# Moving the untaken branch for extra expert blocks one step ahead in a latent-attention and mixture-of-experts kernel

## The chip, the cores and the metric

The kernel runs on one core of a Trainium2 chip. The metric is the device time of one execution in microseconds (us); a value is the median of several runs. PE is TensorE, DVE is VectorE, ACT is ScalarE, POOL is GpSimd, and SP is the queue that mostly issues transfers.

## The reference

The input x has 2 x 4096 tokens of 512 channels in float32. It is normalized without gain, xn = layernorm(x). Two branches read xn, and both are added to x:

```python
x = x + attn(xn) + ffn(xn)

# attn: 64-channel latent attention, causal, one head
c  = (xn @ W_to_kv.T) @ W_compress.T
ch = layernorm(c) * ln_gamma + ln_beta
q, k, v = ch @ W_q_comp.T, *split(ch @ W_kv_comp.T)      # rotary on q and k
o  = softmax(causal(q @ k.T / 8)) @ v
z  = o @ W_comp2lat.T
attn = z @ W_to_kv + z @ W_out_res.T + b_out_res

# ffn: 16 experts, the best 2 for each token, and one shared expert
p   = softmax(xn @ router_w.T); w, e = top_k(p, 2); w = w / sum(w)
ffn = silu(xn @ shared_gate) * (xn @ shared_up) @ shared_down
ffn[token] += w * ((silu(xn @ gate[e]) * (xn @ up[e])) @ down[e])
```

## The kernel before, in words

The kernel has five stages. (1) In 16 groups of 512 tokens it normalizes, routes, computes the shared expert, and projects q, k and v; the rows of xn go to the DRAM buffer xn_d, the shared part to acc_d. (2) It sorts the tokens by expert through DRAM. (3) Attention for six pairs of query blocks (FIRST) runs. (4) The expert stage runs, and within it some scores for a further pair. (5) Attention for the other pairs (REST) runs, together with the summing of all parts into the output.

*The expert stage.* Each token stands twice in the sorted order, which is cut into blocks of 128 rows. There are at most 143 blocks (NBLK): 98 lie in 49 pairs of one expert, the other 45 are single. The last six single blocks (NTAIL) are needed only when the routing is unusually uneven, so they stand inside a branch on a count, `used`. The 137 usual blocks are done in 69 steps (`n_usual`, steps 0 to 68) of two blocks each; as 39 usual singles is an odd number, the last step, 68, has only one block. For step t these helpers are traced:

- `fetch` (three weight transfers of 512 KB each, issued by SP) and `gather_for` (POOL gathers 128 rows of xn_d for each block);
- `x_T`: PE transposes the rows into the PSUM tiles pxt (L1026), DVE copies them to xt and computes the row weight sw (L1029 to L1034);
- `gate_up`: PE multiplies into the PSUM pair pg (L1052), ACT takes silu (esg, L1057), DVE the product (eh, L1058);
- `down`: PE multiplies into the PSUM pair py (L1066), ACT scales the rows by sw into y (L1070) and issues the store to y_d (L1071).

The order on PE, DVE and ACT is the order in which the source traces the work; a scheduler only adds the waits. The loop body is, shortened:

```python
fetch_for(t + 2); gather_for(...); gate_up(t)
...
down(t - 1)
exps(1)                 # a waiting exponential of attention, on ACT
x_T(t + 2)
```

so that `gate_up` of a step always stands ahead of `down` of the step before. After the last `down` every engine loads `used` (L1099) and jumps over the branch (L1101). An untaken branch still ends on each engine with an event by which the others know that it has passed; those that come to a buffer that was used inside the branch wait for it. On SP and POOL that end also waits for earlier transfers.

*Buffers.* PSUM pairs (`psA`) rotate between two buffers and serve pg, py, the scores s and the sums po. In SBUF the pools wx (weights, gathered rows) and ex (a fourth weight buffer, xt, esg, eh, y) are released after the expert stage. In their place come the pool rb for tiles E, which hold rows of scores, and the pool fin for the summing.

*Attention (REST).* For each turn PE transposes pieces of E into the PSUM tiles et (L857), ACT or DVE copies them to eT (L863 to L866), PE multiplies with v into oT (L877); meanwhile PE computes scores s for the next pair (L804), DVE scales them into E and takes the maximum (L812, L809), and ACT takes exponentials in place (L820). Tiles E come from rb, 8 buffers, and when 8 are live from ring_k, 4 buffers. For summing, SP loads acc_d rows into fac (L1141), POOL gathers rows of y_d by position onto fac or into fyy (L1146), and DVE adds (L1167, L1176). These loads and gathers need all stores to y_d.

## Time and profile before

| | |
|---|---|
| runs | 2016.24, 2014.66, 2008.76 us |
| median | 2014.66 us |
| profiled execution | 2016.73 us, its span 2014.9 us |
| mean granted TensorE clock | 0.971 |
| PE busy | 1907.1 us (95%) |
| DVE, ACT, POOL busy | 1057.6, 650.0, 572.9 us |

The profile is of one execution. Its span runs from the first to the last instruction; the time of the run has 1.8 us more. Times in rows count from the span's start. A q behind an engine's name is its sequencer, which waits, branches and issues; "idle before" is the time in which the engine did nothing before the row, with the one that ended it. In these times the expert stage runs up to about 1676, and attention for the other pairs from there to the end.

### The profile page before, as it was taken

How to read it: one execution, taken by the hardware profiler on the slowest of the kernel's cores; microseconds unless marked ns; L12 is line 12 of the kernel's file. 1: busy time of each engine (PE TensorE's matmuls, PEld its weight loads, DVE VectorE, ACT ScalarE, POOL GpSimd, SP SyncE). 2: the span in 40 equal slices, each digit the busy share in tenths (PEclk: the TensorE clock that was granted, in tenths of full speed). 3: DMA queues.
4: the chain of work that ended last, by engine and by line, in shares of the span. 5: the costliest groups of instructions: out<-in, count | busy, mean ns of one | idle time of the engine just before them, and what ended most of it. 6: DMA issues, size and time to landing. Idle time of an engine off the chain costs nothing. (4 is left out here: it accounts for less than half of the span.)

```text
span 2014.9 us, 33391 instructions
## 1 busy us (share of the span) xinstructions
PE 1907.1 (95%) x13010; PEld 1402.0 (70%) x13010; DVE 1057.6 (52%) x2882; ACT 650.0 (32%) x1097; POOL 572.9 (28%) x499
## 2 busy tenths in 40 slices
PE   7999999999999898889999999999999998999997
PEld 6877777777777777467777777777777674444544
DVE  8777777776767677642222322222223315677775
ACT  2222222222222222551111111111111354666665
POOL 2333333333333234101111111111111105555552
PEclk9999999999999998999999999999999999999999
DMA  6221212121212121427887878887877767889885
GB/s 229 63 74 63 74 63 74 64 74 64 74 63 74 64 74 48 147 72 238 271 277 264 300 247 282 281 279 264 276 275 242 243 231 179 216 206 218 201 209 141
DMA packets 219440, 342.50 MB, mean 170 GB/s; under 512 B 19204, under 2 KB 109952, under 8 KB 219280
## 3 DMA queue, kind: packets, MB, share of 16 engines
q1 hardware_dynamic: 167600, 234.09, 35.5%
q0 software_dynamic: 31696, 69.99, 13.8%
q10 hardware_dynamic: 19984, 36.25, 4.7%
q8 instruction: 104, 1.70, 0.4%
q14 instruction: 56, 0.46, 0.1%
HBM read 250.22 MB, written 90.05 MB: 169 GB/s over the span
## 5 line engine op out<-in xcount | busy, mean ns | idle before, releaser
L1052 PE MATMUL pg<-xt,wgu 128*128 128x256 f32 (+1 forms) x2816 | 497.1, 336 | 0.0
L1052 PEld LDWEIGHTS pg<-xt,wgu 128*128 128x128 f32 x2816 | 435.5, 191 | 43.3 <-issue 0.5
L995 POOL DMA_INDIRECT xg<-xn_d,table x137 | 131.4, 959 | 692.7 <-DVE sw L1034 545.5
L1058 DVE TENSOR_TENSOR eh<-esg,pg 128x512 f32<-128x512 f32 (+1 forms) x69 | 47.2, 684 | 399.4 <-ACT esg L1057 393.6
L1066 PE MATMUL py<-wdn,eh 128*128 128x512 f32 x548 | 247.1, 594 | 0.0
L1029 DVE COPY xt<-pxt 128x512 f32<-128x512 f32 x138 | 88.4, 682 | 182.3 <-PE pxt L1026 182.3
L1066 PEld LDWEIGHTS py<-wdn,eh 128*128 128x128 f32 x548 | 102.2, 190 | 106.6 <-issue 98.5
L812 DVE TENSOR_SCALAR_CACHE_REDUCE E<-s 128x512 f32<-128x512 f32 x224 | 144.6, 687 | 58.5 <-PE s L804 39.5
L1070 ACT ACTIVATE y<-py,sw 128x512 f32<-128x512 f32 x137 | 94.2, 688 | 231.4 <-PE py L1066 203.0
L820 ACT ACTIVATE E<-E,nb 128x1024 f32<-128x1024 f32 (+7 forms) x160 | 160.7, 1007 | 20.9 <-DVE nb L815 20.7
L1057 ACT ACTIVATE esg<-pg 128x512 f32<-128x512 f32 (+1 forms) x69 | 41.0, 594 | 370.9 <-PE pg L1052 304.6
L804 PE MATMUL s<-kT,qT 64*128 64x512 f32 (+2 forms) x576 | 144.2, 590 | 16.4 <-DVE E L812 12.6
L877 PE MATMUL oT<-eT,vv 128*64 128x256 f32 (+1 forms) x1088 | 146.7, 392 | 1.4 <-DVE qT L879 0.6
L423 POOL DMA_INDIRECT order_d<-tok,at_u x128 | 126.3, 987 | 64.5 <-issue 36.4
L863 ACT COPY eT<-et 128x512 f32<-128x512 f32 x190 | 104.2, 587 | 110.3 <-PE et L857 63.4
L877 PEld LDWEIGHTS oT<-eT,vv 128*64 128x64 f32 x1088 | 67.3, 138 | 91.5 <-issue 35.0
L857 PEld LDWEIGHTS et<-ident,E 64*128 64x128 f32 x2112 | 81.8, 140 | 70.1 <-issue 49.2
L384 POOL TENSOR_TENSOR x<-x,b_bc 128x2048 f32<-128x2048 f32 x16 | 76.0, 4751 | 186.2 <-DVE xn L381 173.4
L458 PE MATMUL plc<-RC,xnT 128*64 128x80 f32 x1024 | 72.3, 288 | 48.1 <-ACT xnT L447 36.6
L1146 POOL DMA_INDIRECT fyy<-y_d,pos_all x64 | 82.4, 1288 | 121.2 <-PE s L804 54.2
L857 PE MATMUL et<-ident,E 64*128 64x64 f32 x2112 | 101.9, 231 | 15.4 <-ACT E L820 8.4
L1146 POOL DMA_INDIRECT fac<-y_d,pos_all x64 | 98.7, 1541 | 62.2 <-DMA fac<-y_d,pos_all 51.5
(246 smaller groups left out, 2830.2 us busy)
## 6 DMA issues: line engine op xcount, KB each, us to landing
wgu<-in_L_ffn_gate_w_dram SPq DMA_DIRECT2D x88, 512.0 KB
wgu<-in_L_ffn_up_w_dram SPq DMA_DIRECT2D x88, 512.0 KB
wdn<-in_L_ffn_down_w_dram SPq DMA_DIRECT2D x88, 512.0 KB
y_d<-y ACTq DMA_DIRECT2D x137, 256.0 KB
xn_d<-xn SPq DMA_DIRECT2D x16, 1028.0 KB
x<-in_L_attn_x_dram SPq DMA_DIRECT2D x16, 1024.0 KB
acc_d<-x SPq DMA_DIRECT2D x16, 1024.0 KB
fac<-acc_d SPq DMA_DIRECT2D x64, 256.0 KB
```

Source lines behind the costliest of these rows:

```text
L423: G.indirect_dma_start(out=order_d[n % 4], out_offset=bass.IndirectOffsetOnAxis(ap=at_u[:, i, k:k + 1], axis=0), in_=tok[:, g * 4 + i, k:k ...
L804: mm(out=sc[b][:, 0:w], lhsT=q[e, :], rhs=kT[c][e, 0:w], start=True, stop=True)
L812: V.tensor_scalar(dst, sc[b][:, 0:w], SCALE, None, ALU.mult, ALU.max, accum_out=m)
L820: S.activation(E, E, AF.Exp, bias=nb[:, b:b + 1], accum_out=sm[:, b, c:c + 1])
L857: tr(pt[h][:, o:o + H], rows[i][j // 8][e, b, (j % 8) * P:(j % 8 + 1) * P], ident[e, e])
L863: copy(dst[:, h:h + 3:2, :], pt[h].rearrange("p (u c) -> p u c", u=2))
L877: mm(out=o, lhsT=vv[j // 4][:, b, j % 4, :], rhs=e, start=(j == 0), stop=(j == n - 1))
L995: G.indirect_dma_start(out=x_n, out_offset=None, in_=xn_d, in_offset=bass.IndirectOffsetOnAxis(ap=table[:, n:n + 1], axis=0))
L1052: mm(out=pg[:, g, f, at_s], lhsT=weights[u][0][:, c, g * FE + f * P:g * FE + (f + 1) * P], rhs=x_u[:, c, :], start=(c == 0), stop=(c == 3))
L1066: mm(out=py[:, v, :], lhsT=hT[:, c, v * P:(v + 1) * P], rhs=weights[u][1][:, c, :], start=(c == 0), stop=(c == 1))
L1070: S.activation(y, py[:, v, :], AF.Copy, scale=slot_w.pop(n))
L1146: G.indirect_dma_start(out=y, out_offset=None, in_=y_d, in_offset=bass.IndirectOffsetOnAxis(ap=pos[k][:, j:j + 1], axis=0), compute_op=ALU ...
```

## The change

The branch moves into step 68. There, `down(67)` is traced first, then the branch, then `gate_up(68)` and `down(68)`. The branch's six blocks are now six steps of one block instead of three of two. Inside it the weights have a tile tag of their own (wgu_l), and the down weights and transposed rows take tiles of the gathered rows' tag. In step 68 a second block's rows are scaled on DVE and stored by SP. The pool rb of 8 buffers becomes rb of 5 and rc of 3.

```diff
-    tail = [flow[n:n + 2] for n in range(0, len(flow), 2)]
+    tail = [[f] for f in flow]
...
+    def row_tile(name):
+        return wx.tile([P, D + TOPK], F32, tag="xg", name=name, bufs=GBUFS)[:, 0:D]
...
-    def fetch(u):
+    def fetch(u, late=False):
...
-        pool, bufs = (wx, WBUFS) if k < WBUFS else (ex, 1)
-        wgu = pool.tile([P, 4, 2 * FE], F32, tag="wgu", name=f"wgu{u}", bufs=bufs)
-        wdn = pool.tile([P, 2, D], F32, tag="wdn", name=f"wdn{u}", bufs=bufs)
+        pool, bufs = (wx, WBUFS) if k < WBUFS and not late else (ex, 1)
+        wgu = pool.tile([P, 4, 2 * FE], F32, tag="wgu_l" if late else "wgu", name=f"wgu{u}", bufs=bufs)
+        if late:
+            wdn = [row_tile(f"wdn{u}_{c}") for c in range(2)]
+        else:
+            wdn_all = pool.tile([P, 2, D], F32, tag="wdn", name=f"wdn{u}", bufs=bufs)
+            wdn = [wdn_all[:, c, :] for c in range(2)]
...
         def x_T(t):
-            xt = ex.tile([P, 4, 2, P], F32, tag="xt", name=f"xt{t}")
+            xt = (ex.tile([P, 4, 2, P], F32, tag="xt", name=f"xt{t}") if t < n_usual
+                  else row_tile(f"xt{t}").rearrange("p (c v t) -> p c v t", c=4, v=1))
...
                 y = ex.tile([P, D], F32, tag="y", name=f"y{n}", bufs=4)
+                if t == n_usual - 1 and v:
+                    V.tensor_scalar(y, py[:, v, :], slot_w.pop(n), None, ALU.mult)
+                    nc.sync.dma_start(out=y_d[n * P:(n + 1) * P, :], in_=y)
+                    continue
                 S.activation(y, py[:, v, :], AF.Copy, scale=slot_w.pop(n))
                 S.dma_start(out=y_d[n * P:(n + 1) * P, :], in_=y)
+
+        def last_blocks():
+            more_than_usual = nc.values_load(used[0:1, 0:1], min_val=0, max_val=NBLK, ...)
+            with tc.If(more_than_usual > NBLK - NTAIL):
+                for t in range(n_usual, len(steps2)):
+                    for u, _ in steps2[t]:
+                        fetch(u, True)
+                    gather_for(t, True)
+                    x_T(t)
+                    gate_up(t)
+                    down(t)
...
+                if t == n_usual - 1:
+                    down(t - 1)
+                    last_blocks()
                 gate_up(t)
...
-            if t:
+            if t and t != n_usual - 1:
                 down(t - 1)
...
-        more_than_usual = nc.values_load(used[0:1, 0:1], ...)
-        with tc.If(more_than_usual > NBLK - NTAIL):
-            for t in range(n_usual, len(steps2)):
...
-    rb_ = ctx.enter_context(tc.tile_pool(name="rb", bufs=8))
+    rb_ = ctx.enter_context(tc.tile_pool(name="rb", bufs=5))
+    rc_ = ctx.enter_context(tc.tile_pool(name="rc", bufs=3))
...
-        pool = rb_ if sum(t[0] is rb_ for t in live) < 8 else ring_k
+        pool = next(q for q, k in ((rb_, 5), (rc_, 3), (ring_k, 4)) if sum(t[0] is q for t in live) < k)
```

More of the change, by code (lines that the diff above doesn't have):

```diff
@@ L979, in fetch @@
             in_=up_w[bass.ds(e, 1), :, :].rearrange("e (c p) f -> p (e c) f", p=P))
-        nc.sync.dma_start(
-            out=wdn,
-            in_=down_w[bass.ds(e, 1), :, :].rearrange("e (c p) f -> p (e c) f", p=P))
+        if late:
+            for c in range(2):
+                nc.sync.dma_start(
+                    out=wdn[c], in_=down_w[bass.ds(e, 1), c * P:(c + 1) * P, :].rearrange("e p f -> p (e f)"))
+        else:
+            nc.sync.dma_start(
+                out=wdn_all,
+                in_=down_w[bass.ds(e, 1), :, :].rearrange("e (c p) f -> p (e c) f", p=P))
         weights[u] = wgu, wdn
@@ L1065, in down @@
                 for c in range(2):
-                    mm(out=py[:, v, :], lhsT=hT[:, c, v * P:(v + 1) * P], rhs=weights[u][1][:, c, :],
+                    mm(out=py[:, v, :], lhsT=hT[:, c, v * P:(v + 1) * P], rhs=weights[u][1][c],
                        start=(c == 0), stop=(c == 1))
@@ L1069, in down @@
                 y = ex.tile([P, D], F32, tag="y", name=f"y{n}", bufs=4)
+                if t == n_usual - 1 and v:
+                    V.tensor_scalar(y, py[:, v, :], slot_w.pop(n), None, ALU.mult)
+                    nc.sync.dma_start(out=y_d[n * P:(n + 1) * P, :], in_=y)
+                    continue
                 S.activation(y, py[:, v, :], AF.Copy, scale=slot_w.pop(n))
                 S.dma_start(out=y_d[n * P:(n + 1) * P, :], in_=y)
+        def last_blocks():
+            more_than_usual = nc.values_load(used[0:1, 0:1], min_val=0, max_val=NBLK,
+                                             skip_runtime_bounds_check_because="a sum of block counts that cannot exceed NBLK")
+            with tc.If(more_than_usual > NBLK - NTAIL):
[6 more added lines that the diff above has]
+                    down(t)
         rows, todo = score_steps(E_first, NPA, two_banks)
@@ L1096, in tile_mla_then_moe @@
                 (offsets_of_tokens if t == 20 else slots)()
-        more_than_usual = nc.values_load(used[0:1, 0:1], min_val=0, max_val=NBLK,
-                                         skip_runtime_bounds_check_because="a sum of block counts that cannot exceed NBLK")
-        with tc.If(more_than_usual > NBLK - NTAIL):
-            for t in range(n_usual, len(steps2)):
-                for u, _ in steps2[t]:
-                    fetch(u)
-                gather_for(t, True)
-                x_T(t)
-                gate_up(t)
-                down(t)
     on_way.__exit__(None, None, None)
-    rb_ = ctx.enter_context(tc.tile_pool(name="rb", bufs=8))
+    rb_ = ctx.enter_context(tc.tile_pool(name="rb", bufs=5))
+    rc_ = ctx.enter_context(tc.tile_pool(name="rc", bufs=3))
     fin = ctx.enter_context(tc.tile_pool(name="fin", bufs=2))
```

## The prediction

> **What bounds the kernel now.** I read the page's busy row first, then everything that names the branch's line, then PE, ACT and DVE in order of time around it. Columns of a timeline row: start, length, engine, line, operation, count, and in brackets the idle time before it and what ended it.

> ```profile
> PE 1907.1 (95%) x13010; PEld 1402.0 (70%) x13010; DVE 1057.6 (52%) x2882; ACT 650.0 (32%) x1097; POOL 572.9 (28%) x499
> L1070 ACT ACTIVATE y<-py,sw 128x512 f32<-128x512 f32 x137 | 94.2, 688 | 231.4 <-PE py L1066 203.0
> ```

> TensorE is the bound: time is won or lost only where PE stands. The second row counts 137 scaled row blocks, all 143 but the last six, so the branch is not taken in this run: only its test and its joining are paid.

> ```profile
> L1101 SPq EVENT_SEMAPHORE  x9: 17/17/17, 1653.8 to 1678.1; - x9
> ...
> L1101 DVEq COMPARE_BRANCH  x1: 72/72/72, 1670.1 to 1670.1; - x1
> ...
> L1101 PEldq COMPARE_BRANCH  x1: 3346/3346/3346, 1670.6 to 1670.6; - x1
> ...
> L1101 ACTq EVENT_SEMAPHORE  x1: 17/17/17, 1676.6 to 1676.6; - x1
> ...
>   DVE E L812: 8.4, 1
> ```

> PE's jump took 3346 ns, DVE's 72. SP comes out of the branch only at 1678.1, ACT at 1676.6, and DVE had to wait for SP.

> ```profile
> 1661.89 3.60 PE L1066 MATMUL py<-wdn,eh 128*128 128x512 f32 x8
> 1665.33 3.73 PE L1052 MATMUL pg<-xt,wgu 128*128 128x128 f32 x32
> 1668.90 5.32 PE L1066 MATMUL py<-wdn,eh 128*128 128x512 f32 x12
> 1674.36 0.83 PE L857 MATMUL et<-ident,E 64*128 64x64 f32 x16
> 1676.67 1.99 PE L804 MATMUL s<-kT,qT 64*128 64x512 f32 x8 [1.48 <-ACTq L1101]
> ...
> 1691.13 1.36 PE L804 MATMUL s<-kT,qT 64*128 64x384 f32 x4 [3.94 <-DVE E L812]
> ```

> The last expert step (69th, numbered 68) has one block: its pg is 128x128, its py 4 of the 12 matmul records. PE's jump at 1670.6 is hidden, because py matmuls already handed over run to 1674.2. After the transposes PE stands 1.48 us for ACT's join.

> ```profile
> 1665.53 0.69 ACT L1070 ACTIVATE y<-py,sw 128x512 f32<-128x512 f32 x1 [2.84 <-PE py L1066]
> 1666.62 0.69 ACT L1070 ACTIVATE y<-py,sw 128x512 f32<-128x512 f32 x1 [0.41 <-ACT y L1070]
> ...
> 1674.79 0.69 ACT L1070 ACTIVATE y<-py,sw 128x512 f32<-128x512 f32 x1 [0.48 <-ACT y L1070]
> ...
> 1669.51 0.42 DVE L1058 TENSOR_TENSOR eh<-esg,pg 128x256 f32<-128x256 f32 x1 [6.10 <-ACT esg L1057]
> ...
> 1678.32 0.69 DVE L812 TENSOR_SCALAR_CACHE_REDUCE E<-s 128x512 f32<-128x512 f32 x1 [8.38 <-SPq L1101]
> ...
> 1689.17 0.69 DVE L863 COPY eT<-et 128x512 f32<-128x512 f32 x1 [4.04 <-remote]
> ...
> 1678.93 0.95 POOL L1146 DMA_INDIRECT fyy<-y_d,pos_all  x1 [54.16 <-PE s L804]
> ...
> 1689.00:1693.00 4.00, 1.86 (x8) 0.69 (x10) 3.60 (x10) 1.87 (x2) 2.66 (x3) 0.81 1.10 265
> ```

> (The last line is of the windows view: busy time of PE, PE's weight loads, DVE, ACT and POOL in the stretch, then TensorE's granted clock.)

> Attention proper starts with DVE at 1678.32. So the stretch that the change touches is 1665 to 1678, of which PE loses about 1.5 us and DVE, behind it, some 0.5 more (s is ready 1.18 us after its start, by the s at 1682.64 and its E at 1683.82: 1677.85).

> **The change, part by part.** In the instruction lists of both programs all engines run the same order up to step 68 and again from the first transposes of attention on. What differs lies between.

> *Row scaling on two engines.* The new DVE path needs a second block in step 68. There is none (the 128x128 row), so no DVE scaling and no SP store is issued: 0. Were it used, it could save no more than one ACT row and its gap, 1.09 us (1666.62 - 1665.53), and cost no more than that on DVE.

> *The branch, moved.* Before, PE's order is pg68, py67, py68, branch, attention; after, py67, branch, pg68, py68, attention. Call PE's end of py66 1665.4 in both.
> - py67 takes the place of pg68: 1665.33 + 3.60 = 1668.93. Its input was ready long before (pg67 ended at 1662.05).
> - ACT scales py67's two blocks: 0.04 after its end (as at 1665.53, where py66 ended at 1665.49), 1.09 to the second, 0.69: 1670.75. Each issues its y store, inside the 1.09. Then ACT tests and joins: before, from the last y's end 1675.48 to PE's release at 1676.67, 1.19. That gives 1671.94.
> - pg68 now has a wait that it had not: its PSUM pair was last used inside the branch, by ACT, so it starts at ACT's join, as s did before. PE stands from 1668.93 to 1671.94, 3.01 us. Behind pg68 on PE are py68, all transposes and all scores.
> - py68 needs silu and product of pg68. Before, py67 covered that chain; now nothing stands between. From pg68's start to the product's end was 1665.33 to 1669.93, 4.60: 1676.54. The second stall, about 0.9 us, is new.
> - py68 is 5.32 - 3.60 = 1.72: 1678.26. Transposes 0.83: 1679.09. s starts there, no join ahead of it; first E on DVE 1.18 later: 1680.27.

> Against 1678.32 that is **+1.95 us**. What goes: the 1.48 of PE and DVE's wait for SP. What comes: 3.0 and 0.9.

> *PE's jump, and a rule.* The row says 3.35 us, and from PE's load of the count (1670.0) to its next weight load (1674.33) 4.3 us. [...] By the row, PE reaches it between 1663.4 (py67's input ready) and 1665.4 and is through by 1667.7 to 1669.7, still ahead of ACT's 1671.94: also 0. If PE reached it only when py67 has run, 1668.93 + 4.3 = 1673.2 gives +1.3 more. I take the row and 0, and keep 1.3.

> *TensorE's clock, and a rule against this change.* Behind the 3.94 us of idle PE before 1691.13 the granted clock in the stretch 1689 to 1693 was 0.81; in each stretch of 4 us from 1665 to 1689 it was 1.00. [...] I take 0 and keep 0 to 1.7.

> *SP and POOL.* Their tests keep their place in the two queues (before: POOL 1624, SP 1653). SP's join now waits for y67's stores, not y68's. But the loads of acc_d (SP) and the gathers of y_d (POOL) need y68's store: gathers started 4.14 after y68's scaling began; 1678.3 + 4.14 is 1682.4, +3.5 us. Behind them wait only DVE's sums, first at 1708.7, 30 us later; no wait for a DMA among DVE's waits from 1690 on. 0; if that cover were gone, 3.5 in place of 1.95, as the shifts overlap.

> *Tiles.* The branch's own tiles (wgu_l, and row tiles for wdn and xt) are used only inside it: 0. The E tiles' pool of 8 becomes 5 and 3, 12 with the old ring as before. A reused E tile is freed by PE's transposes, and its new scores stand behind those on PE, so DVE waits no longer than for the scores: 0. The trace can't show it; from both sides by a nearby row, one E row of 0.69, gain or loss.

> *Not explained.* From 1685.2 to 1689.17 DVE and ACT waited for the third turn's transposes with a releaser that the profile doesn't name, 4.0 us, behind the old join. Nothing in the change removes it by what I see; it may go (-4.0) or be met twice (+4.0). I take 0.

> Sum: +1.95. The profiled execution took 2016.73 (span 2014.9 and 1.8 around it), 2.07 above the median, which lies inside 2008.76 to 2016.24. On the median: 2014.66 + 1.95 = **2016.6**.

> **The rivals.**
> 1. *The stall behind the join goes* (faster side). It sits in attention's third turn, as buffers and transfers start together (gathers from 1678.93); if the later gathers or the absent SP join part them, 4.0 us of waiting and up to 1.7 of half clock go: 1.95 - 5.7 = -3.75, 2010.9. It decides once more than half of the 4.0 goes. For it: it occurs just there, and nowhere later in that stage. Against: gathers move with attention (+3.5 and +1.95), so the same things meet again.
> [...]
> 3. *Nothing*: joins trade places evenly, 2014.7. For it: the same instructions; against: pg68's new wait on ACT and the bare silu chain.

> **How the numbers follow.** My case 0.45, rival 1 0.22, rival 2 0.25, rival 3 0.08. A difference of 0.5%, 10.1 us, is about what a measurement of this kernel can tell from no change; runs alone spread over 7.5. All centres lie within it. Past it lie only tails, where a shift at this seam is handed on to more than one turn of attention, in which PE, DVE and ACT wait for each other all the time: that I can't price, and give it 0.35, which makes the rest, 0.65, within. Of the 0.35, 0.21 go to slower, since my sum and rival 2 point there, and 0.14 to faster, with rival 1. The range reaches from rival 1 with the spread below its centre (2010.9 - 3.9) to rival 2 with the stall (2023.6) and as much: 2007 to 2027. My own case alone: 2012 to 2021.

> **What would show it.** Right: in the new profile pg68 (128x128) waits about 3 us for ACT's branch line, py68 about 1 us for the product, s follows the transposes at once, no DVE wait for SP's branch line, PE's branch still over 3 us but hidden, no y on DVE. Wrong: pg68 starts at once behind py67; the third turn's 4 us are gone; PE's clock falls in the stretch behind pg68's wait; DVE's sums wait for gathers; or the difference lies outside these 15 us altogether.

## The result, and the profile after

| | before | after |
|---|---|---|
| median of 22 runs each | 2013.68 us | 2020.89 us |
| range | 2008.76 to 2020.29 | 2013.88 to 2028.03 |
| profiled execution, its span | 2016.73, 2014.9 us | 2021.18, 2019.5 us |
| mean granted TensorE clock | 0.971 | 0.970 |

The ratio is 1.0031, with a 95% interval of 1.0021 to 1.0040: 6.2 us slower (4.2 to 8.1), less than the 0.5% that the prediction takes for what a measurement of this kernel can tell from no change, and more than the 1.95 that its sum gave. (The two medians themselves differ by 7.2; the text goes by the ratio, which has an interval.) The two spans differ by 4.6.

The busy row of the page after is nearly the one before (PE 1907.1): nothing was added that computes.

```profile
PE 1908.3 (94%) x13010; PEld 1405.3 (70%) x13010; DVE 1055.9 (52%) x2882; ACT 650.3 (32%) x1097; POOL 571.2 (28%) x499
```

Next come the rows of PE in order of time (start, length, engine, line, operation, count, idle time before it and what ended it). L1080 is `down`, L1066 `gate_up`, L1095 the branch.

```profile
1661.76 7.03 PE L1080 MATMUL py<-wdn,eh 128*128 128x512 f32 x16
1671.85 6.71 PE L1066 MATMUL pg<-xt,wgu 128*128 128x128 f32 x32 [3.06 <-ACTq L1095]
1679.54 1.98 PE L1080 MATMUL py<-wdn,eh 128*128 128x512 f32 x4 [0.98 <-DVE eh L1072]
1681.46 0.71 PE L857 MATMUL et<-ident,E 64*128 64x64 f32 x16
1682.01 1.94 PE L804 MATMUL s<-kT,qT 64*128 64x512 f32 x8
...
1696.09 1.65 PE L804 MATMUL s<-kT,qT 64*128 64x384 f32 x4 [4.07 <-DVE E L812]
```

The order is as foretold: `down` of steps 66 and 67 in one row, a stall of 3.06 for ACT's join, pg of step 68, a stall of 0.98 for the product, py, and then transposes and scores without a stop. Of those the length of pg stands out: 6.71 us for the 32 matmuls that took 3.73 before. The rows of ACT, DVE and POOL, and the branch's line, bear out the rest:

```profile
1668.83 0.69 ACT L1088 ACTIVATE y<-py,sw 128x512 f32<-128x512 f32 x1 [1.66 <-PE py L1080]
...
1669.98 0.69 ACT L1088 ACTIVATE y<-py,sw 128x512 f32<-128x512 f32 x1 [0.46 <-ACT y L1088]
...
1679.07 0.42 DVE L1072 TENSOR_TENSOR eh<-esg,pg 128x256 f32<-128x256 f32 x1 [15.79 <-ACT esg L1071]
1683.14 0.69 DVE L812 TENSOR_SCALAR_CACHE_REDUCE E<-s 128x512 f32<-128x512 f32 x1 [3.65 <-PE s L804]
...
1694.13 0.69 DVE L863 COPY eT<-et 128x512 f32<-128x512 f32 x1 [4.18 <-remote]
...
1685.16 0.95 POOL L1170 DMA_INDIRECT fyy<-y_d,pos_all  x1 [60.53 <-ACT eT L863]
```

```profile
L1095 PEldq COMPARE_BRANCH  x1: 3346/3346/3346, 1663.9 to 1663.9; - x1
...
L1095 ACTq EVENT_SEMAPHORE  x1: 17/17/17, 1671.8 to 1671.8; - x1
...
  PE pg L1066: 3.1, 1
```

The first E now waits for its scores and no longer for SP. Between the product's row (1679.07) and the first E stands no y on DVE. The list of those who waited for the branch names pg and its weight load only. The windows view gives the reason for the 6.71 (busy times of PE, its weight loads, DVE, ACT, POOL; then the granted clock, the DMA share and GB/s):

```profile
1669.00:1673.00 4.00, 1.15 (x5) 1.15 (x6) 0.00 (x0) 1.20 (x2) 0.00 (x0) 0.76 0.38 139
1673.00:1677.00 4.00, 4.00 (x21) 4.00 (x20) 0.00 (x0) 0.00 (x0) 0.00 (x0) 0.50 0.00 0
1677.00:1681.00 4.00, 3.02 (x14) 2.05 (x13) 0.42 (x1) 0.39 (x1) 0.00 (x0) 0.89 0.00 0
```

Lost clock, each stretch times what its clock lacks to 1.00: 4 x (0.24 + 0.50 + 0.11) = 3.4 us, that is 6.8 us at half speed. Before, every stretch from 1665 to 1689 had 1.00.

Positions are compared as distances from the start of `down` of step 66 to the first E of attention. Before it is 1678.32 - 1661.89 = 16.43 us, after 1683.14 - 1661.76 = 21.38. That is **+4.95**, made of the predicted +1.95 and 3.0 more; pg alone is 6.71 - 3.73 = 2.98 longer. The median's +6.2 has 4.95 in its interval, and 1.95 not.

So the theory to be tested: (a) the branch's place costs about 2 us by its two stalls, less the one it removes; (b) the gap in front of pg also brings the clock down, which costs up to 3 us more. Rivals: the tiles and pool sizes cost it; PE's jump costs it; or the low clock would have come there without the gap.

### The profile page after: what moved, and what is told of

Read it like the earlier page. It is cut to its first block, busy times and chain, and to the rows that moved or that the text cites. A ratio compares the mean times of both kernels' runs of the same rounds, so it can differ in the third digit from the quotient of the medians.

```text
span 2019.5 us, 33396 instructions
## 1 busy us (share of the span) xinstructions
PE 1908.3 (94%) x13010; PEld 1405.3 (70%) x13010; DVE 1055.9 (52%) x2882; ACT 650.3 (32%) x1097; POOL 571.2 (28%) x499
## 3 DMA queue, kind: packets, MB, share of 16 engines
q8 instruction: 105, 1.72, 0.4%
## 5 line engine op out<-in xcount | busy, mean ns | idle before, releaser
L1066 PE MATMUL pg<-xt,wgu 128*128 128x256 f32 (+1 forms) x2816 | 500.2, 337 | 3.1 <-ACTq L1095 3.1
L1066 PEld LDWEIGHTS pg<-xt,wgu 128*128 128x128 f32 x2816 | 438.4, 192 | 46.8 <-ACTq L1095 3.9
L1080 PE MATMUL py<-wdn,eh 128*128 128x512 f32 x548 | 247.2, 594 | 1.0 <-DVE eh L1072 1.0
L1080 PEld LDWEIGHTS py<-wdn,eh 128*128 128x128 f32 x548 | 102.2, 190 | 107.8 <-issue 98.5
L812 DVE TENSOR_SCALAR_CACHE_REDUCE E<-s 128x512 f32<-128x512 f32 x224 | 144.4, 686 | 52.3 <-PE s L804 46.8
L1088 ACT ACTIVATE y<-py,sw 128x512 f32<-128x512 f32 x137 | 94.2, 687 | 232.1 <-PE py L1080 204.1
L804 PE MATMUL s<-kT,qT 64*128 64x512 f32 (+2 forms) x576 | 144.4, 590 | 14.6 <-DVE E L812 12.3
L863 ACT COPY eT<-et 128x512 f32<-128x512 f32 x190 | 104.2, 587 | 107.3 <-PE et L857 58.7
L857 PEld LDWEIGHTS et<-ident,E 64*128 64x128 f32 x2112 | 81.7, 140 | 69.3 <-issue 48.6
L857 PE MATMUL et<-ident,E 64*128 64x64 f32 x2112 | 101.8, 231 | 14.8 <-ACT E L820 8.1
```

What stands on the lines that cost most here:

```text
L804: mm(out=sc[b][:, 0:w], lhsT=q[e, :], rhs=kT[c][e, 0:w], start=True, stop=True)
L812: V.tensor_scalar(dst, sc[b][:, 0:w], SCALE, None, ALU.mult, ALU.max, accum_out=m)
L857: tr(pt[h][:, o:o + H], rows[i][j // 8][e, b, (j % 8) * P:(j % 8 + 1) * P], ident[e, e])
L863: copy(dst[:, h:h + 3:2, :], pt[h].rearrange("p (u c) -> p u c", u=2))
L1066: mm(out=pg[:, g, f, at_s], lhsT=weights[u][0][:, c, g * FE + f * P:g * FE + (f + 1) * P], rhs=x_u[:, c, :], start=(c == 0), stop=(c == 3))
L1080: mm(out=py[:, v, :], lhsT=hT[:, c, v * P:(v + 1) * P], rhs=weights[u][1][c], start=(c == 0), stop=(c == 1))
```

## Experiments

They ran on three chips, whose times of the kernel before differ: chip A (2019.13 us, near the first measurement), B (1951.98) and C (1934.02). Ratios and distances are therefore taken only against the kernel before on the same chip, and the profile of before, which is of the first measurement, is compared by distances. Each variant's median is of 12 runs, that of before on the same chip of 29 or 35.

| run | chip | ratio to before, 95% | py66 to first E | pg of step 68 |
|---|---|---|---|---|
| before (first measurement) | | | 16.43 | 3.73 |
| after (first measurement) | | 1.0031 (1.0021 to 1.0040) | 21.38 | 6.71 |
| again | A | 1.0020 (1.0006 to 1.0033) | 21.28 | 6.62 |
| gap5 | A | 1.0033 (1.0018 to 1.0049) | 22.17 | 6.54 |
| mid | A | 1.0024 (1.0007 to 1.0041) | 18.74 | 3.73 |
| midfill | A | 1.0022 (1.0007 to 1.0036) | 19.87 | 3.73 |
| a_end | B | 1.0005 (0.9990 to 1.0021) | 16.48 | 3.73 |
| fill1 | B | 1.0018 (1.0000 to 1.0036) | 18.50 | 3.84 |
| fill3 | B | 1.0009 (0.9993 to 1.0025) | 18.50 | 3.84 |
| dve67 | B | 1.0011 (0.9994 to 1.0028) | 18.98 | 5.47 |
| same_after | C | 1.0025 (1.0010 to 1.0041) | 20.00 | 5.33 |
| same_fill3 | C | 1.0018 (1.0006 to 1.0031) | 18.50 | 3.84 |
| same_end | C | 1.0004 (0.9988 to 1.0020) | 16.45 | 3.73 |

In every row the distance less 16.43, as a share of the time, lies inside the interval of the ratio: what is lost at this seam is what shows in the time, as far as the runs can tell.

### a_end: all of the change but the branch's place

```diff
-                if t == n_usual - 1:
-                    down(t - 1)
-                    last_blocks()
                 gate_up(t)
...
-            if t and t != n_usual - 1:
+            if t:
                 down(t - 1)
...
+        last_blocks()
```

> The changed kernel with its branch put back behind the last down step; the branch's own tiles, its single-block steps and the pools of 5 and 3 stay. Theory A (the place of the branch costs: a wait for ACT's join, a bare silu chain, and half clock behind the gap): as before, 2013.7 us within 2, pg of the last step back at 3.7 us with no wait, first E of attention about 1678.3 in the trace. Rival C (the tiles or the split pools cost): about 2020, first E still near 1678 but the loss later in attention.

Measured: ratio 1.0005, distance 16.48, and the old waits are back, ACT's join for the scores and SP's for DVE. PE and DVE in order of time:

```profile
1604.48 5.32 PE L1080 MATMUL py<-wdn,eh 128*128 128x512 f32 x12
...
1612.26 1.99 PE L804 MATMUL s<-kT,qT 64*128 64x512 f32 x8 [1.43 <-ACTq L1095]
...
1613.96 0.69 DVE L812 TENSOR_SCALAR_CACHE_REDUCE E<-s 128x512 f32<-128x512 f32 x1 [8.44 <-SPq L1095]
```

The branch's own tiles, its six single steps and the split of rb cost nothing that shows at this seam or in the time (whose interval is -2 to +4 us). What the change costs is the place of the branch.

### fill3 and fill1: the gap covered, wholly and in part

Unused multiplications of 128x512 stand on PE between the branch and pg: three in fill3, one in fill1.

```diff
                     last_blocks()
+                    cover = psO("cover")
+                    for _ in range(3):
+                        mm(out=cover, lhsT=ident, rhs=mask, start=True, stop=True)
                 gate_up(t)
```

> The changed kernel with three more matmuls of 128x512 on PE between the branch and gate_up of the last step; their result is not used. They need no join of ACT, take about 2.7 us, and so lie in the 3.06 us in which PE stood. Theory A: the clock stays up, pg of the last step takes 3.7 us instead of 6.71, start unchanged at about 1671.9, first E 3.0 us earlier than in the changed kernel, time 2017.9. Rival B (the slow pg has another cause, or the low clock comes with the phase of the clock's windows whatever PE does): pg still about 6.7, time 2020.9.

> As fill3 with one extra matmul, about 0.9 us, which leaves a gap of some 2.1 us. Theory A: if the length of the gap decides, the clock stays up here too, pg 3.7 us, 2017.9; if any gap of some 2 us can still drop it, pg lies between 3.7 and 6.7 and the time between 2017.9 and 2020.9. Rival B: as the changed kernel, 2020.9.

PE in fill3, and its clock around the filler and pg:

```profile
1597.67 7.03 PE L1080 MATMUL py<-wdn,eh 128*128 128x512 f32 x16
1604.85 2.81 PE L1122 MATMUL cover<-mask,ident 128*128 128x512 f32 x6
1607.76 3.84 PE L1066 MATMUL pg<-xt,wgu 128*128 128x128 f32 x32
1612.58 1.98 PE L1080 MATMUL py<-wdn,eh 128*128 128x512 f32 x4 [0.98 <-DVE eh L1072]
```

```profile
1607.00:1612.00 5.00, 4.50 (x34) 3.65 (x32) 0.00 (x0) 0.32 (x1) 0.00 (x0) 1.00 0.16 59
```

The same row for fill1, where 1.81 of the gap was left:

```profile
1610.22 3.84 PE L1066 MATMUL pg<-xt,wgu 128*128 128x128 f32 x32 [1.81 <-ACTq L1095]
```

Pg starts at the same distance from py66 in both as in the changed kernel (1607.76 - 1597.67 = 10.09, and 10.09 again in fill1; after: 1671.85 - 1661.76 = 10.09). So ACT's join sets it, whether PE idles or not. Only the clock differs: 1.00 and 3.84 us for pg. Both distances are 18.50, +2.07 over before. That is the prediction's sum, 1.95, with its clock. The filler also shows that PE's jump was over by then: multiplications behind the branch began 0.15 us after the last py (1604.85 against 1597.67 + 7.03 = 1604.70).

### dve67: a shorter gap by scaling step 67's second block on DVE

```diff
-                if t == n_usual - 1 and v:
+                if t == n_usual - 2 and v:
                     V.tensor_scalar(y, py[:, v, :], slot_w.pop(n), None, ALU.mult)
```

> The changed kernel with the row scaling on DVE and the store on SP moved from the last step, which has no second block, to the step before, which has one. ACT then has one row block less ahead of its join. Theory A: ACT's join comes 1.1 us earlier (1670.7), PE's gap shrinks from 3.06 to about 2.0, and if the clock stays up the time is 2020.9 - 1.1 - 3.0 = 2016.8, otherwise 2019.8. Rival B: 2019.8. A rival to the join itself (PE waits for its own jump, which took 3346 ns, not for ACT): no change of pg's start, 2020.9.

PE's rows and DVE's, then the clock:

```profile
1602.91 5.47 PE L1066 MATMUL pg<-xt,wgu 128*128 128x128 f32 x32 [1.92 <-ACTq L1095]
...
1601.75 0.75 DVE L1085 TENSOR_SCALAR y<-py,sw 128x512 f32<-128x512 f32 x1 [6.27 <-ACT y L1088]
```

```profile
1603.00:1608.00 5.00, 5.00 (x31) 5.00 (x32) 0.00 (x0) 0.00 (x0) 0.00 (x0) 0.66 0.21 77
```

The gap shrank by 1.14 (3.06 to 1.92), close to the 1.09 of an ACT row with its gap. This is what scaling on two engines brings where a second block exists. But the clock still fell: 5 x 0.34 = 1.7 us lost, 3.4 at half speed, and pg took 5.47. **A gap of 1.92 us was enough**, while fill1's 1.81 was not; the reason is read below, under same_after.

### again and gap5: the changed kernel repeated, and with a longer gap

gap5 delays ACT's join by three unused copies.

```diff
                     down(t - 1)
+                    for _ in range(3):
+                        S.copy(ex.tile([P, 2 * 2 * P], F32, tag="sg", name="delay"), mask)
                     last_blocks()
```

> The changed kernel itself once more, beside the kernel before on this chip. In the profile of fill1 and dve67 gaps of 1.8 and 1.9 us met a low clock in one and not in the other, so a gap of 3 us should meet one in some executions and not in others. Theory A: pg of the last step waits 3.06 us for ACT's join and py 0.98 for the product; pg takes 3.7 to 6.7 us by the clock it meets; time above before by 2 (no low clock) to 5 us (all of pg at half clock), 0.10 to 0.25%. Rival D (the whole +6 of the first measurement belongs to the chip on which it was taken, where PE also stood 4 us in attention's third turn): no difference here.

> The changed kernel with three copies of 128x512 more on ACT between the last scaled rows and ACT's test of the count (their result is not used). They delay ACT's join by about 1.8 us, so PE's gap grows from 3.06 to about 4.9 us. Theory A: pg starts 1.8 us later, and so long a gap drops the clock in nearly every execution, for 6.8 us: 1.8 + up to 3.0 above the changed kernel, 5 to 7 us above before (0.25 to 0.35%). If ACT's join is not what PE waits for: as the changed kernel.

The row of pg in again, then in gap5:

```profile
1674.43 6.62 PE L1066 MATMUL pg<-xt,wgu 128*128 128x128 f32 x32 [3.06 <-ACTq L1095]
```

```profile
1672.11 6.54 PE L1066 MATMUL pg<-xt,wgu 128*128 128x128 f32 x32 [4.02 <-ACTq L1095]
```

again repeats the first result: 3.06, 6.62, distance 21.28, and the ratio's interval lies above 1, here and in same_after, on a chip without that third-turn stall: rival D falls. In gap5 the copies took 1.66 us on ACT, but the gap grew only by 0.96, not by the expected 1.8, and the distance by about as much (22.17 - 21.28 = 0.89). A gap of 4.02 costs no more clock than one of 3.06: in both 6.8 us at half speed.

### mid and midfill: the branch between gate and up of step 68 and down of step 67

Here pg of step 68 runs before the branch, as in the kernel before. In midfill two unused multiplications stand behind the branch (the three lines on `cover` below).

```diff
-            h = ex.tile([P, 2, 2 * P], F32, tag="h", name=f"eh{t}")
+            h = (ex.tile([P, 2, 2 * P], F32, tag="h", name=f"eh{t}") if t < n_usual
+                 else row_tile(f"eh{t}").rearrange("p (g s) -> p g s", g=2))
...
+                gate_up(t)
                 if t == n_usual - 1:
-                    down(t - 1)
                     last_blocks()
-                gate_up(t)
+                    cover = psO("cover")
+                    for _ in range(2):
+                        mm(out=cover, lhsT=ident, rhs=mask, start=True, stop=True)
+                    down(t - 1)
```

> The changed kernel with the branch between gate_up of the last step and down of the step before, and a tile of its own for the branch's product. ACT has then no scaled rows ahead of its join but those of two steps before and one silu, and both down steps stand together behind the branch, which cover the silu chain. Theory A: PE's gap at the branch about 1.7 us (ACT's join 1.1 us behind its silu of the last step), no second gap, s follows the transposes at once; first E about 0.4 us earlier than before: as before within 0.1%, or up to 1.7 us more where the gap meets a low clock. If the place ahead of the end costs in itself, whatever ACT has queued: as the changed kernel.

> As mid, with two matmuls of 128x512 on PE behind the branch, whose result is not used, in the gap of about 1.7 us. Theory A: they fit into the gap, which vanishes, PE's clock stays up, time 0.4 us below before; too small to be told from no change in the times, so the trace decides: first E relative to the end of py of step 66 at 12.5 us, against 12.9 in the kernel before.

mid: PE's row behind the branch, and two rows of the branch's line (engine, operation, length in ns, start in us):

```profile
1672.51 6.95 PE L1081 MATMUL py<-wdn,eh 128*128 128x512 f32 x12 [3.02 <-PEq L1096]
```

```profile
L1096 PEldq COMPARE_BRANCH  x1: 3886/3886/3886, 1668.2 to 1668.2; - x1
L1096 ACTq COMPARE_BRANCH  x1: 54/54/54, 1670.1 to 1670.1; - x1
```

midfill, PE's filler:

```profile
1672.80 3.47 PE L1123 MATMUL cover<-mask,ident 128*128 128x512 f32 x4 [2.48 <-PEq L1096]
```

Here the releaser is PEq, and not ACT's join as expected (with a gap of 1.7): PE waits for its own jump, begun at 1668.2 and through at 1672.1, 2 us after ACT had passed. With so little work handed over ahead of it (pg ends at 1669.5) the jump lies bare. In midfill the filler stood behind the jump too, so it could not fill the gap, as was expected, but was added to it. Both clocks fell again for 3.4 us, behind 3.02 and 2.48. The py rows of mid took 6.95 where 5.32 is their time at full clock; without those 1.63 the distance would be 17.1, 0.7 over before.

### same_after, same_fill3 and same_end: three versions on one chip

> The changed kernel unaltered, beside the two next runs on one chip, since the versions with a covered gap and with the branch at the end have been timed only on another chip than the changed kernel. Theory (the branch costs about 2 us in its place, and the half clock behind its gap about 3 us more): start of py66 to the first E 21.3 us, gate and up of step 68 at 6.6 to 6.7 us behind a gap of 3.06, time 4 to 6 us over before. Rival (the cost depends on the chip): on a chip without the late transposes gate and up of step 68 run at full clock behind the same gap, 3.7 to 3.9 us, and the distance is 18.5.

> The changed kernel with three unused multiplications of 128x512 between the branch and gate and up of step 68 (their result is used by nothing). Theory: gate and up of step 68 at 3.7 to 3.9 us on this chip too, distance from py66 to the first E 18.5, so about 2.8 us less than the changed kernel on the same chip, about 2 over before. Rival (the filler only moves the low clock to later work, or the cost lies elsewhere): the distance falls, but the time stays at the changed kernel's.

> The changed kernel with the branch back behind the last down, its own tiles and pool sizes kept. Theory: distance from py66 to the first E 16.4, time equal to before within 0.2%, and about 5 us under the changed kernel on the same chip. Rival (tiles and pool sizes cost part of it where the chip shows the late transposes): 2 us or more over before.

The row of pg in same_after, its clock, and the row of pg in same_fill3:

```profile
1592.46 5.33 PE L1066 MATMUL pg<-xt,wgu 128*128 128x128 f32 x32 [3.06 <-ACTq L1095]
```

```profile
1588.80:1592.21 3.41, 0.60 (x2) 0.00 (x0) 0.00 (x0) 1.37 (x2) 0.00 (x0) 1.00 0.39 145
1592.21:1595.63 3.42, 3.17 (x15) 3.17 (x16) 0.00 (x0) 0.00 (x0) 0.00 (x0) 0.50 0.21 75
1595.63:1599.04 3.41, 2.43 (x20) 2.24 (x20) 0.42 (x1) 0.38 (x1) 0.00 (x0) 1.00 0.00 0
```

```profile
1594.12 3.84 PE L1066 MATMUL pg<-xt,wgu 128*128 128x128 f32 x32
```

On one chip the three stand in the theory's order: 16.45 with the branch at the end, 18.50 with the gap covered, 20.00 as changed. The expected 21.3 was missed for same_after. The clock lost 3.42 x 0.50 = 1.7 us, one stretch of 3.4 at half speed and not two, so pg took 5.33. The rival, full clock on this chip, fell as well. The times are 1.0004, 1.0018 and 1.0025: the same order, with same_fill3 and same_after too close for their intervals to part (1.2 to 6.0 us over before, and 1.9 to 7.9). The share of the clock rests on the rows, not on the medians. That the filler only moves the low clock to later work is not what the profiles show: same_fill3 has one low stretch 35.6 us behind its first E, where same_after has none, but same_end, without a filler, has one too, 34.6 behind.

**Where the low stretches begin.** The kept profiles together say what decides whether a gap brings the clock down. In each of the thirteen the clock is 1.00 or 0.50, and all its falls (6 to 24 in a profile) lie on one grid of 3.413 us: the time between any two of them is a whole multiple of that, to 0.004 us, over the whole 1.9 to 2.0 ms. So a profile can be cut into windows from one point of the grid to the next, as same_after is above. In the same cut after (three windows), dve67 (two) and fill1 (two):

```profile
1667.67:1671.09 3.42, 1.12 (x3) 0.19 (x1) 0.00 (x0) 1.37 (x2) 0.00 (x0) 1.00 0.43 158
1671.09:1674.50 3.41, 2.65 (x12) 2.65 (x13) 0.00 (x0) 0.00 (x0) 0.00 (x0) 0.50 0.23 83
1674.50:1677.91 3.41, 3.41 (x18) 3.41 (x17) 0.00 (x0) 0.00 (x0) 0.00 (x0) 0.50 0.00 0
```

```profile
1600.70:1604.11 3.41, 1.50 (x11) 1.21 (x11) 0.75 (x1) 0.69 (x1) 0.00 (x0) 1.00 0.50 183
1604.11:1607.53 3.42, 3.42 (x18) 3.42 (x17) 0.00 (x0) 0.00 (x0) 0.00 (x0) 0.50 0.02 5
```

```profile
1605.83:1609.24 3.41, 2.42 (x6) 0.56 (x4) 0.00 (x0) 1.37 (x2) 0.00 (x0) 1.00 0.42 150
1609.24:1612.66 3.42, 2.44 (x21) 2.44 (x22) 0.00 (x0) 0.00 (x0) 0.00 (x0) 1.00 0.30 108
```

The clock falls behind a window in which PE was busy for too small a share: 0.18 in same_after, 0.33 in after, 0.44 in dve67. The gap of dve67 lies whole in one window. That of fill1, shorter by only 0.11 us, is cut by the grid into 0.83 and 0.98, which leaves both windows 0.71 busy, and nothing falls. Over all thirteen profiles, from the first record of the clock on (22.35 us into the span in that of before), every window at full clock with PE busy under 0.42 was followed by one at half clock, and none above 0.64; between, both occur. The second low stretch of after fits as well: the grid cuts its 3.06 us into 2.30 and 0.76, so that PE was busy for only 0.78 of the first low window. In same_after 0.25 us fell into that window, it was 0.93 busy, and one stretch was all. The second condition is not settled, though: in the early stages of gap5 and mid a second low window follows some that are fully busy. The shares are approximate, as a profile models where matmuls end. And all this is read from profiles after the fact; no run set a gap at a chosen point of the grid.

No version tried beats the kernel before. Those with the branch at its end equal it.

## Why the prediction was right or wrong

- *TensorE's clock*: **the step that failed.** It took 0 and kept 0 to 1.7. No run shows 0 behind this gap, nor 1.7 as the most that the clock can cost there; both were the author's estimates. Measured: 2.98 in the first profile, 2.89 in again, 1.60 in same_after; only with the gap covered near 0 (3.84 against 3.73). Gaps of 1.92, 2.48, 3.02 and 3.06 us each brought the clock down to 0.50. What goes with a fall, by the windows above, is how busy PE was in one window of 3.4 us, and not the length of a gap alone. The profile of before could have told: the prediction read one of its 21 falls, and eleven of the others come behind windows in which PE was idle for no more than 1.8 us in all (1.41 in the two rows at the end of this point). The lost clock itself comes in whole stretches of 3.4 us at 0.50: at the branch 3.4 us (same_after, dve67, mid, midfill) or 6.8 (the first profile, again, gap5) in every run that has any. One stretch loses 3.4 x 0.50 = 1.7, two in a row 3.4. The two windows of before:

```profile
889.33:892.75 3.42, 2.01 (x31) 1.28 (x25) 2.12 (x7) 0.06 (x1) 0.00 (x0) 1.00 0.72 228
892.75:896.16 3.41, 3.09 (x21) 2.60 (x21) 2.75 (x11) 0.00 (x0) 1.76 (x2) 0.50 0.80 254
```

- *The branch, moved*: right to a tenth. The first stall was 3.06 for 3.01, the second 0.98 for 0.9, pg's start at 10.09 behind py66 for 10.05. With the clock up, the whole step is +2.07 (fill3, fill1), or +2.05 against same_end on chip C, for +1.95.
- *PE's jump*: right. It took 3346 ns, began at 1663.9, and lay under py67, so the kept 1.3 was not needed. (DVE's took 72 ns, those of SP, POOL and ACT 50 to 58.) That it can show was right to keep: in mid it did.
- *SP and POOL*: right that it is hidden. The gathers started 6.4 us later, counted from py66 (1685.16 - 1661.76 for 1678.93 - 1661.89; 3.5 was predicted, and the clock adds 3.0). DVE's waits from 1680 to the end, with time in total, times and longest, begin so, and no DMA is among them:

```profile
DVE E L812 <- PE s L804: 38.2, 37, 3.6
DVE eT L863 <- PE et L857: 25.5, 18, 4.4
DVE fac L1191 <- PE po L1187: 21.7, 18, 2.3
DVE eT L863 <- remote: 4.2, 1, 4.2
```

- *Tiles*, and *row scaling on two engines*: 0, as predicted (distances of 16.48 in a_end and 16.45 in same_end for 16.43; no y on DVE).
- *Not explained*, and rival 1: the third turn's stall stayed, 4.18 for 4.04, so the faster side fell. On chips B and C it is absent whatever the branch's place (0.65 us before the same scores row in same_after, and in a_end and same_end with the old join), so it does not come from the old join.
- Rival 2, on the slower side, had the clock fall behind the gap and the jump show. The first came true and the second didn't. Its sum, 1.95 + 1.3 + 1.7 = +4.95, equals the measured distance by chance: the 1.3 for the jump cost nothing, and for the 1.7 the clock cost 3.0.
- The direction was right, and the median after, 2020.89, lies in the range given. The size was off by the one term: 1.95 + 3.0 = 4.95, where the measured 6.2 has an interval of 4.2 to 8.1.

Left open: where between 0.42 and 0.64 of busy time the line runs, and what a second low stretch needs in general. A gap of 1.81 us whole in one window would leave it 0.47 busy, so whether it drops the clock is not shown either.

## What to carry to other kernels

The join moved off one path landed on another here: stalls of 3.06 and 0.98 us came for the 1.48 that went. So price the stall that appears where a join goes, with all that is queued behind it, and not only the one that leaves. Idle gaps on TensorE of 1.92 to 4.02 us in otherwise full stretches made the work behind them 1.6 to 3.0 us longer here (pg 5.33 to 6.71 us for 3.73, and py 6.95 for 5.32 in mid), and one of 1.81 did not (pg 3.84 in fill1): price such a gap in this kernel at its length plus as much, until a profile shows the clock staying up. Which end of that range comes can differ between executions of one kernel: in three profiles of the changed one the last grid point before pg lay 0.76, 0.96 and 0.25 us ahead of it, and pg took 2.98, 2.89 and 1.60 us longer. And place a jump behind enough work already handed over to its engine: behind a `down` the jump of 3.35 us left no idle time on PE in before and after, and that of 3.67 left 0.20 us in a_end; in mid, where pg of step 68 alone stood before it, the jump of 3.89 set a gap of 3.02 us.
